# Transposes in two forms: full, or on two row halves, with two PSUM banks each, in a scheduled macaron layer

## Chip, cores and metric

The kernel runs on one core of a Trainium2 chip. The metric is the device time of one execution in microseconds (us); the times shown are medians of several runs. Profiles come from one further execution, recorded by the hardware profiler.

## What is computed

The input x is 8 sequences of 512 tokens and 256 features, in float32. Cut to what matters, the reference is:

```python
def _layer(x, ...):                        # feed-forward half, 2 layers deep
    h = shift_token(x); qkv = h @ wqkv     # 8 heads of 64
    q = l2norm(q) * qs; k = l2norm(k) * ksc; q, k = rotary_xpos(q, k)
    o = local_attention(q, k, v)           # window 128, looks one window back
    x = x + o @ wo
    h = layernorm(shift_token(x)) * lg + lb
    a, g = split(h @ w1 + b1)
    return x + (a * gelu(g)) @ w2 + b2

x = x + 0.5 * ffn(layernorm(x))
x = x + attn(layernorm(x))     # h = LN(x); for each token: y = W q; W -= lr (W k - v) k^T; returns LN(x) + y
x = x + 0.5 * ffn(layernorm(x))
```

Here `ffn` applies `_layer` twice. The same `ffn` weights serve both halves.

## The kernel before

Tokens lie on the 128 partitions: a sequence is four tiles of 128 tokens by 256 features. For each of the 8 sequences and each half and layer, a tile w of x is normalised where a norm is due, transposed on TensorE so that features lie on the partitions (`h.turn`, two 128x128 transposes into one PSUM bank), copied to SBUF (`h.copy`, `hT`), and multiplied with wqkv (L690 for q and k, L777 for v). q and k are rotated (L734, L740, L746) and transposed head by head (`qk.turn`, L801), scores are made (L841), exponentials and shares taken (L896, L917), the shares transposed (`pr.turn`, L943), weighed with v (L980) and projected (L1031). The feed-forward step shifts tokens by DMA into `hs`, normalises two tiles together, transposes them with four 128x128 transposes into one bank (`hn.turn`), spreads them to `h2T` with a scale and a bias on ScalarE (L1102), and multiplies with w1 (L1124) and w2 (L1215, L1226). Between the halves, `ttt` solves the token recurrence in blocks; its normalised rows go through `zn.turn`, two transposes, and a spread (L1304).

All three turns (`h.turn`, `hn.turn`, `zn.turn`) come from one helper, `transposes`, whose instructions all have line L638. There are 128 + 64 + 32 = 224 such steps with 576 transposes in all.

TensorE works in one of three forms, which the code calls kinds: `full` (all 128 rows and columns), `rows` (two halves of 64 rows that work side by side, each into a bank of its own: `qk.turn`, `pr.turn`, L1226 and some steps of `ttt`) and `quad` (four quarters of 64x64: scores, weighing, and the blocks of L1424). The turns of L638 are `full`.

Nothing runs in the order of the source. Each step becomes a `Node` with engine, cost, kind, the buffers that it takes (`Val`, from pools; the pool `ps` is the eight PSUM banks) and those that it uses. `Scheduler.run` (L361) then writes out the instructions of all engines, one node after the other: of all nodes that are ready and for which `room` finds free buffers, it takes the one with the smallest time by its own costs, less a tuned head start (`EARLY` by name, and a pseudo-random one by `VARIED`, one number for each 10 us of TensorE's clock). A node may name several engines (`copy` on ACT or DVE), and then the scheduler picks one; a change of TensorE's kind has its own costs (`PE_DRAIN`, `PE_LOAD`). A value with a `mate` gets two neighbouring banks where it can, and `both_of` returns a view of both. Each engine executes its own instructions in the order written.

At the start, `load_x` (L495) loads a sequence's x; that of sequence 0 goes in four pieces of one tile each, the first ahead of the identity `sq`. The weights' rope tables are multiplied with the scales (L536), each product on DVE or POOL, whichever the scheduler picks; it picked one on each.

Of the kernel before, what the change touches and what calls it, by code (L numbers as in the profile page):

```python
# [112 lines left out]
def t_pool(n, spread=False):  # L113
# [5 lines left out]
    "XT": 400,  # L119
    "XT6": 200,  # L120
    "_full_quad": 850,
    "_full_rows": 350,
    "_quad_full": 400,
    "_quad_rows": 450,
    "_rows_full": 500,
    "_rows_quad": 650,
    "_table": -250,
    "base.x": -700,
    "base.y": 50,
    "base.z": -550,  # L130
    "below": -250,
    "block": 1000,
    "bx": 500,
    "bx.copy": -450,
    "bx6": 1000,
    "bx6.copy": -1000,
    "cross.mask": 2000,
    "down": -300,
    "exp": -950,
    "g": 1000,  # L140
    "gate": 400,
    "gelu": -450,
    "gram": -50,
    "gram.copy": -750,
    "h.copy": -1650,
    "h.edge": 2100,
    "h.turn": 200,
    "h2T": -800,
    "hn": 350,
    "hn.turn": 250,  # L150
    "hs.rstd": -1350,
    "hs.stats": 100,
    "hs.zero": -400,
    "k.scale": 2350,
    "keys": -200,
    "keys.copy": -300,
    "kq": 5100,
    "kq.copy": -1000,
    "last": 200,
    "last.gelu": -650,  # L160
    "least": -250,
    "norm 0": 100,
    "norm 1": 400,
    "ones": 2100,
    "po": 3300,
    "po.add": 50,
# [3 lines left out]
    "pred": 500,  # L170
# [4 lines left out]
    "qk.power": -1650,  # L175
    "qk.square": -550,
    "qk.sum": -550,
    "qk.swapped": 2800,
    "qk.turn": 5050,
    "recip": 950,  # L180
    "remains": 650,
    "rest": -200,
    "rope": -2950,
    "sc": 2350,
    "sequence 4": 350,
    "shares": -50,
    "start": 1000,
    "tv": 2350,
    "u": 5500,
    "u.copy": -100,  # L190
    "v": -50,
    "value": 150,
    "w": 4650,
    "w.add": 350,
    "x.ffn": 200,
    "x.rstd": -1900,
    "x.scale": -500,
    "x.stats": 500,
    "xbx": 2650,
    "xbx.t": 500,  # L200
    "xbx6": 1000,
    "y": 300,
    "z.rstd": -400,
    "z.scale": 50,
    "z.stats": 5600,
    "zT": -450,
    "zero": -1000,
    "zn.rstd": -1850,
    "zn.scale": -350,
    "zn.stats": -500,  # L210
    "zn.turn": 4500,
# [6 lines left out]
    11724, 1019, 59022, 40675, 27471, 54517, 926, 43545, 2398, 24437, 2885, 26297, 23063, 34949,  # L218
    37569, 50685, 32060, 45684, 31371, 39512, 521, 25144, 9512, 57341, 52812, 27993, 489, 16985,
    33884, 26540, 4908, 18540, 8984, 2421, 40841, 59716, 24566, 55621, 54901, 36686, 11720, 16862,  # L220
    12513, 52674, 46515, 10256, 59276, 45325, 19184, 55405, 46136, 42422, 0, 49317, 40524, 44024,
    17428, 31920, 9589, 43511, 59281, 2218, 23017, 28209, 39306, 27771, 33355, 29993, 985, 13712,
    12640, 23397, 12680, 25585, 54109, 44131, 30596, 53412, 59847, 58748, 23508, 2544, 28302, 26557,
    42944, 35720, 53117, 52196, 48722, 45182, 35154, 35344, 11332, 52827, 37344, 43276, 41480,
    25425, 12724, 27463, 8460, 45364, 1608, 2076, 43844, 20601, 2037, 2469, 59305, 53718, 46665,
    7337, 2226, 52207, 33281, 58457, 21599, 41269, 26533, 7438, 10800, 59668, 36328, 9166, 3745,
    46520, 33573, 21192, 14896, 27355, 52409, 47920, 36060, 3581, 40705, 14777, 12200, 5106, 3270,
    51090, 49236, 40806, 56120, 57783, 44110, 54754, 7737, 4795, 57152, 33780, 10581, 19156, 33936,
    14061, 55609, 27768, 30248, 49510, 51041, 20100, 12337, 22860, 5369, 43128, 56887, 21496, 42396,
    49657, 59934, 54949, 51695, 25315, 48261, 6245, 14319, 39121, 50043, 51556, 33881, 37401, 54689,  # L230
    49233, 9924, 153, 33064, 19456, 55060, 55649, 39006, 35496, 52294, 57662, 8411, 23088, 13299,
    21788, 20784, 0, 45292, 52752, 9077, 52413, 35269, 49088, 4635, 56036, 34956, 34764, 55744,
    11631, 10468, 37148, 21711, 44697, 28554, 26398, 22219, 1471, 23536, 6706, 44201, 48828, 45578,
    39704, 45276, 44363, 20013, 25017, 14320, 36906, 53273, 39761, 9386, 19064, 51436, 46401, 15636,
    47446, 53601, 57004, 17096, 7331, 58485, 46128, 47692, 33874, 15433, 23706, 38397, 0, 31180,
    20101, 11661, 56899, 1609, 28145, 25749, 31949, 39204, 1318, 18757, 46711, 24881, 52292, 1629,
    38037,
# [57 lines left out]
class Node:  # L295
    def __init__(self, name, groups, prio, eng, cost, emit, deps, takes, uses, kind, tail, port):
        self.name, self.early = name, sum(EARLY.get(k, 0.0) for k in (name, *groups))
        self.groups, self.key = groups, zlib.crc32(f"{name} {prio[0]}".encode())
        self.prio, self.cost, self.emit, self.takes, self.kind = prio, cost, emit, takes, kind
        self.engs = eng if isinstance(eng, tuple) else (eng,)  # L300
        self.costs = cost if isinstance(cost, tuple) else (cost,)
        self.uses, self.next, self.ready, self.tail, self.port = uses, [], None, tail, port
        self.banks = [v for v in self.uses if v.tag == "ps"]
        self.left = 0
        for d in deps:
            d.next.append(self)
            self.left += 1
        self.deps = deps
        for v in uses:
            v.users += 1  # L310


class Scheduler:
# [47 lines left out]
    def run(self):  # L361
        ready = [n for n in self.nodes if n.left == 0]
        left = len(self.nodes)
        while left:
# [3 lines left out]
            for n in ready:  # L368
# [5 lines left out]
                for eng, cost in zip(n.engs, n.costs):  # L374
# [4 lines left out]
                    if eng == "PE":  # L379
                        t += PE_LOAD[n.kind]  # L380
                        if self.pe_kind not in (n.kind, None):
                            now += PE_DRAIN[self.pe_kind] + PE_LOAD[n.kind]
                            turn = f"_{self.pe_kind}_{n.kind}"
                    elif eng == "ACT" and n.kind and n.kind != self.table:
# [3 lines left out]
                    key = (t - early + EARLY.get(turn, 0.0) + (cost if len(n.engs) > 1 else 0.0), n.prio)  # L388
                    if best is None or key < best[0]:
                        best = (key, n, eng, cost, t, turn)  # L390
            assert best, f"no node can go: {left} left, " + str({k: len(v) for k, v in self.free.items()})
            _, n, eng, cost, t, turn = best
            ready.remove(n)
            left -= 1
            n.ran = eng
# [7 lines left out]
            if eng == "PE":  # L403
                self.pe_kind = n.kind
            if eng == "ACT" and n.kind:
                self.table = n.kind
# [16 lines left out]
def macaron_kernel(ctx: ExitStack, tc: tile.TileContext, a: dict, out: bass.AP):  # L423
# [71 lines left out]
    def load_x(b, w=None):  # L495

        if not w:
            lane[b], first_x[b] = Val("lane"), Val("x")
        own = slice(0, NW) if w is None else slice(w, w + 1)
        order[0] += 1  # L500
        n = node(
# [3 lines left out]
            1500.0 if w is None else 790.0,  # L505
            lambda e: dma(first_x[b].ap[:, own, :], a["x"][b].rearrange("(w p) d -> p w d", p=P)[:, own, :]),
            takes=[] if w else [lane[b], first_x[b]],
            uses=[first_x[b]] if w else [],
            tail=2200.0,
        )  # L510
        L["x", b] = [n] * NW if w is None else [*L.get(("x", b), []), n]
# [8 lines left out]
    def load_layer(l):  # L520
        wqkv = wpool.tile([P, 2, 3 * INNER], F32, name=f"wqkv{l}")
        load(("qk", l), (wqkv[:, :, 0 : 2 * INNER], split(a["wqkv"][l][:, 0 : 2 * INNER])))
        if l == 0:
# [10 lines left out]
            ("DVE", "POOL"),  # L534
            (t_dve(4 * NW * DH), 2400.0),
            lambda e: (nc.vector if e == "DVE" else nc.gpsimd).tensor_tensor(  # L536
# [1220 lines left out]
```

## Time and profile before

| what | value |
|---|---|
| median of 3 runs | 2679.28 us (2678.38 to 2680.19) |
| profiled execution, its own time | 2681.69 us |
| its span | 2679.9 us |
| TensorE busy (PE) | 98% of the span |
| DVE / ACT / POOL busy | 69% / 62% / 58% |
| granted TensorE clock, mean | 0.999 |
| L638, all turns: busy time and count | 44.8 us for the 256 of x, 40.9 us for the 256 of hs, 12.2 us for the 64 of the recurrence's rows |
| L801, turns of q and k on row halves | 91.8 us, 2048 instructions |

The span runs from the first to the last instruction of the program; the rest of the execution's time lies around it. PE is TensorE's matmuls and transposes, PEld its weight loads, DVE the vector engine, ACT the scalar engine, POOL GpSimd, SP the engine that issues the DMAs. An fp32 matmul of the program appears as two instructions in the trace, a transpose as one. Durations of neighbouring matmuls overlap, so their mean is longer than the time from one start to the next. In a row of the order of time, "[0.57 <-DVE row L1556]" means that the engine was idle for 0.57 us until DVE's work on `row` at L1556 was done.

### The profile page before, as it was taken

How to read it: one execution, taken by the hardware profiler on the slowest of the kernel's cores; microseconds unless marked ns; L12 is line 12 of the kernel's file. 1: busy time of each engine (PE TensorE's matmuls, PEld its weight loads, DVE VectorE, ACT ScalarE, POOL GpSimd, SP SyncE). 2: the span in 40 equal slices, each digit the busy share in tenths (PEclk: the TensorE clock that was granted, in tenths of full speed). 3: DMA queues.
4: the chain of work that ended last, by engine and by line, in shares of the span. 5: the costliest groups of instructions: out<-in, count | busy, mean ns of one | idle time of the engine just before them, and what ended most of it. 6: DMA issues, size and time to landing. Idle time of an engine off the chain costs nothing.

```text
span 2679.9 us, 75965 instructions
## 1 busy us (share of the span) xinstructions
PE 2635.3 (98%) x30128; PEld 1995.6 (74%) x30128; DVE 1846.5 (69%) x5571; ACT 1650.8 (62%) x4342; POOL 1543.8 (58%) x2153
## 2 busy tenths in 40 slices
PE   8999999999999999999999999999999999999998
PEld 4777777777767777777777777777777777777776
DVE  6767757765777667766776777776777756776755
ACT  5666665755666666666565666657656656556554
POOL 7655655654576466656565656457556645456633
PEclk9999999999999999999999999999999999999999
DMA  5000000000100000000000000000010000000000
GB/s 184 9 9 16 7 6 17 11 6 6 32 6 10 8 24 17 8 8 9 8 29 8 10 9 24 18 8 8 9 30 8 10 7 8 9 24 8 8 13 17
DMA packets 58554, 44.61 MB, mean 17 GB/s; under 512 B 7468, under 2 KB 55768, under 8 KB 58200
## 3 DMA queue, kind: packets, MB, share of 16 engines
q1 hardware_dynamic: 58200, 39.77, 4.8%
q8 instruction: 237, 3.88, 0.6%
q14 instruction: 117, 0.96, 0.1%
HBM read 18.79 MB, written 4.19 MB: 9 GB/s over the span
## 4 chain that ended last, share of the span: by engine, by line
PE 92%; DVE 2%; DMA 2%; POOL 2%; ACT 1%; issue 1%; SPq 0%; DVEq 0%; POOLq 0%; ACTq 0%
PE ps L1124 22%; PE ps L690 17%; PE ps L1215 9%; PE ps L1031 8%; PE ps L777 8%; PE ps L841 6%; PE ps L980 6%; PE ps L943 4%; PE ps L801 3%; PE ps L638 3%; PE ps L1424 2%; PE ps L1226 1%; PE ps L1336 1%; DMA hs<-x 1%; PE ps L1568 1%
## 5 line engine op out<-in xcount | busy, mean ns | idle before, releaser
L1124 PE MATMUL ps<-h2T,w 128*128 128x256 f32 (+1 forms) x2816 | 646.1, 381 | 2.6 <-DVE gT L1165 1.3
L1124 PEld LDWEIGHTS ps<-h2T,w 128*128 128x128 f32 (+1 forms) x2816 | 521.3, 188 | 122.5 <-issue 30.6
L690 PE MATMUL ps<-wqkv,hT 128*128 128x512 f32 x1024 | 490.2, 603 | 1.4 <-DVE x L1349 1.1
L896 ACT ACTIVATE pr<-pr,s 128x192 f32<-128x192 f32 (+1 forms) x1024 | 440.4, 433 | 49.9 <-DVE s L884 45.8
L917 POOL TENSOR_TENSOR pr<-pr,s 128x384 f32<-128x384 f32 (+1 forms) x375 | 293.5, 790 | 283.9 <-DVE s L909 260.8
L726 POOL TENSOR_TENSOR st<-st,powc 128x8 f32<-128x8 f32 x256 | 438.2, 1712 | 21.3
L884 DVE CUSTOM_DVE_ANT_0 pr<-ps,amask,st 128x192 f32<-128x192 f32 (+1 forms) x1024 | 360.8, 394 | 44.4 <-PE ps L841 36.0
L911 POOL TENSOR_TENSOR s<-s,powc 128x2 f32<-128x2 f32 x189 | 133.7, 708 | 342.5 <-ACT pr L896 341.2
L1165 DVE SCALAR_TENSOR_TENSOR gT<-ps,b,gl 128x256 f32<-128x256 f32 x320 | 151.0, 482 | 219.6 <-PE ps L1124 189.1
L690 PEld LDWEIGHTS ps<-wqkv,hT 128*128 128x128 f32 x1024 | 185.4, 191 | 154.5 <-issue 137.0
L1215 PE MATMUL ps<-w,gT 128*128 128x256 f32 x1280 | 291.4, 379 | 0.3 <-DVE s L884 0.3
L1215 PEld LDWEIGHTS ps<-w,gT 128*128 128x128 f32 x1280 | 241.6, 190 | 50.8 <-issue 15.3
L709 ACT ACTIVATE tmp<-ps 128x512 f32<-128x512 f32 x256 | 152.4, 597 | 174.0 <-DVE rot L734 127.0
L734 DVE TENSOR_TENSOR rot<-ps,rt 128x512 f32<-128x512 f32 x256 | 175.7, 688 | 117.4 <-PE ps L690 103.8
L1031 PE MATMUL ps<-wo,oT 128*128 128x256 f32 x1024 | 244.0, 381 | 0.5 <-DVE oT L1024 0.5
L777 PE MATMUL ps<-wqkv,hT 128*128 128x512 f32 x512 | 240.5, 594 | 0.0
L1031 PEld LDWEIGHTS ps<-wo,oT 128*128 128x128 f32 x1024 | 190.7, 190 | 51.2 <-issue 19.2
L602 ACT COPY prT<-ps 128x512 f32<-128x512 f32 (+1 forms) x364 | 176.9, 548 | 58.6 <-PE ps L943 56.5
L1146 ACT ACTIVATE gl<-ps,b 128x256 f32<-128x256 f32 x320 | 140.8, 473 | 105.9 <-PE ps L1124 101.1
L841 PE MATMUL ps<-kT,qT 64*64 64x128 f32 (+1 forms) x7168 | 194.2, 251 | 9.7 <-ACT qT L602 8.3
L980 PE MATMUL ps<-prT,v 64*64 64x128 f32 (+1 forms) x7168 | 197.1, 247 | 6.1 <-DVE prT L602 2.9
L746 POOL TENSOR_TENSOR rot<-rot,tmp 128x512 f32<-128x512 f32 x146 | 185.4, 1273 | 19.6 <-DVE tmp L740 14.8
(123 smaller groups left out, 4372.5 us busy)
## 6 DMA issues: line engine op xcount, KB each, us to landing
hs<-x SPq DMA_DIRECT2D x128, 64.0 KB
hs<-x SPq DMA_DIRECT2D x128, 63.5 KB
base<-in_x_dram SPq DMA_DIRECT2D x8, 512.0 KB
out_dram<-base SPq DMA_DIRECT2D x8, 512.0 KB
w<-in_w_dram SPq DMA_DIRECT2D x6, 640.0 KB
x<-in_x_dram SPq DMA_DIRECT2D x7, 512.0 KB
wqkv<-in_wqkv_dram SPq DMA_DIRECT2D x2, 1024.0 KB
hs<-x SPq DMA_DIRECT2D x96, 0.5 KB
```

The source lines that it names most:

```text
L690: nc.tensor.matmul(pp.ap, hT[w].ap[:, c * P : (c + 1) * P], wqkv[:, c, i * INNER : (i + 1) * INNER], start=(c == 0), stop=(c == 1),)
L726: nc.gpsimd.tensor_tensor(ss, ss, powc[:, 0:HEADS], ALU.pow)
L746: (nc.vector if e == "DVE" else nc.gpsimd).tensor_tensor(rot.ap, rot.ap, tmp.ap, ALU.add)
L777: nc.tensor.matmul(pv.ap, hT[w].ap[:, c * P : (c + 1) * P], wqkv[:, c, 2 * INNER : 3 * INNER], start=(c == 0), stop=(c == 1),)
L841: nc.tensor.matmul(sc[par].ap[half(c), k * 4 * DH + at : k * 4 * DH + at + keys.stop - keys.start], qT.ap[half(par), 2 * g + k, half(c)], ...
L884: nc.vector.tensor_tensor_reduce(out=pr(k, nj), in0=sc.ap[:, k * 4 * DH : k * 4 * DH + nj], in1=amask[:, 0:nj] if w else amask[:, 3 * DH : ...
L896: nc.scalar.activation(pr(k, nj), pr(k, nj), AF.Exp, bias=st.ap[:, k : k + 1], scale=-1.0, accum_out=st.ap[:, 2 + k : 3 + k],)
L917: (nc.vector if e == "DVE" else nc.gpsimd).tensor_tensor(both, both, st.ap[:, 4:6].unsqueeze(2).to_broadcast([P, 2, nj]), ALU.mult)
L980: nc.tensor.matmul(po[r].ap[half(par), k * P + first : k * P + first + cols * DH], v[j].ap[half(r), hd * DH : (hd + 1) * DH], prT.ap[half( ...
L1031: nc.tensor.matmul(py.ap[:, 0:D], oT.ap[:, c, :], wo[:, c, :], start=(c == 0), stop=(c == INNER // P - 1))
L1124: nc.tensor.matmul(dst.ap[0:rows, 0 : 2 * P], w1[:, kc, col : col + rows], h2T.ap[:, kc, :], start=(kc == 0), stop=(kc == 1),)
L1215: nc.tensor.matmul(py.ap[:, 0:D], gT.ap[:, at : at + P], w2[:, c, :], start=(c == 0), stop=False)
```

## The change

1. `transposes` takes two banks as mates and has two ways, `("full", "rows")`. In the full way it issues the same 128x128 transposes, half of them into each bank. In the rows way each transpose becomes two, of 64 rows and 128 columns, into the same columns of the two banks. `Node` holds a list of ways (engine, cost, kind) in place of engines and costs, and `run` picks one when it issues the node; `n.ran` tells which. The readers (`h.copy` and the two spreads) read both banks, in the order that the way asks for, when they are issued.
2. `load_x` loads every sequence in one piece, and the call for sequence 0 now follows the identity's.
3. The rope products are on POOL alone.
4. `EARLY` and `VARIED` have new values, so the order on every engine differs throughout.

In the order that results, 75 of the 224 turns go on row halves: 35 of 128 `h.turn`, 33 of 64 `hn.turn` and 7 of 32 `zn.turn`. The sequences are worked through in the order 4, 3, 7, 0, 2, 5, 1, 6, where it was 4, 0, 1, 2, 3, 6, 7, 5; SP issues the inputs of 7, 3 and 4 first, where it was that of 4, then weights, then the four pieces of 0.

```diff
 EARLY = {
...
-    "_full_quad": 850,
-    "_full_rows": 350,
-    "_quad_full": 400,
-    "_quad_rows": 450,
-    "_rows_full": 500,
-    "_rows_quad": 650,
+    "_full_quad": 1050,
+    "_full_rows": 750,
+    "_quad_full": 250,
+    "_quad_rows": 500,
+    "_rows_full": 450,
+    "_rows_quad": 550,
...
-        self.engs = eng if isinstance(eng, tuple) else (eng,)
-        self.costs = cost if isinstance(cost, tuple) else (cost,)
+        ways = [w if isinstance(w, tuple) else (w,) for w in (eng, cost, kind)]
+        count = max(map(len, ways))
+        self.ways = list(zip(*(w * count if len(w) < count else w for w in ways)))
...
-                for eng, cost in zip(n.engs, n.costs):
+                for way in n.ways:
+                    eng, cost, kind = way
...
-            n.ran = eng
+            n.ran = kind
...
-            lambda e: dma(first_x[b].ap[:, own, :], a["x"][b].rearrange("(w p) d -> p w d", p=P)[:, own, :]),
+            lambda e: dma(first_x[b].ap, a["x"][b].rearrange("(w p) d -> p w d", p=P)),
...
-            ("DVE", "POOL"),
-            (t_dve(4 * NW * DH), 2400.0),
+            "POOL",
+            2400.0,
...
-        def transposes(name, dst, src, deps, takes, uses, n):
-            def emit():
+        def transposes(name, pts, src, deps, takes, uses, n):
+            pts[0].mate = pts[1]
+            def emit(e):
+                out = both_of(*pts)
                 for k in range(n):
-                    nc.tensor.transpose(dst(k), src(k), ident)
-            return pe(name, t_tr(times=n), emit, deps, takes=takes, uses=uses)
+                    if me.ran == "full":
+                        nc.tensor.transpose(out[:, 2 * k // n, 2 * k % n * DH : (2 * k % n + 2) * DH], src(k), ident)
+                    else:
+                        for r in range(2):
+                            rows = slice(r * DH, (r + 1) * DH)
+                            nc.tensor.transpose(out[:, r, k * DH : (k + 1) * DH], src(k)[rows], ident[rows, rows])
+            me = node(
+                name, prio(), "PE", (t_tr(times=n), T_TURN * n), emit, deps, [*pts, *takes], uses, ("full", "rows")
+            )
+            return me
...
+                def turned_x(n=n, pts=pts):
+                    src = both_of(*pts)[:, :, 0:P]
+                    return src if n.ran == "full" else src.rearrange("p r (c t) -> p r c t", c=2)
...
-        load_x(0, 0)
         load("ident", (sq, a["sq"]))
-        for w in range(1, NW):
-            load_x(0, w)
+        load_x(0)
```

## The prediction

> **What bounds the kernel now.** I read the page's engine rows first, then the busy time by stretches, then the order of time on TensorE, in the middle of the run and at its start.
>
> ```profile
> span 2679.9 us, 75965 instructions
> ...
> PE 2635.3 (98%) x30128; PEld 1995.6 (74%) x30128; DVE 1846.5 (69%) x5571; ACT 1650.8 (62%) x4342; POOL 1543.8 (58%) x2153
> ```
>
> TensorE is idle for 2679.9 - 2635.3 = 44.6 us in all, and no other engine is above 69%. So the time is TensorE's own stream plus a few waits. Where the waits lie is in the table of stretches (length, busy time of PE, PEld, DVE, ACT, POOL, then granted clock, DMA share, GB/s):
>
> ```profile
> 0.00:60.00 60.00, 48.01 (x439) 26.68 (x440) 40.09 (x125) 28.63 (x83) 46.79 (x80) 0.97 0.60 203
> ...
> 1200.00:1800.00 600.00, 599.54 (x6868) 457.35 (x6861) 425.96 (x1284) 377.92 (x1002) 338.28 (x468) 1.00 0.05 13
> ...
> 2600.00:2680.00 80.00, 69.77 (x798) 53.88 (x796) 44.76 (x134) 34.54 (x98) 29.77 (x38) 0.98 0.05 15
> ```
>
> The first 60 us hold 12.0 us of idle time; the last matmul ends at 2674.6, so 5.3 us at the end are the last additions and the store; 44.6 - 12.0 - 5.3 = 27.3 us are spread over the body. Next is what the stream is made of (start us, duration, instruction; I subtract starts of neighbours, since durations overlap):
>
> ```profile
> 667.41 0.60 PE L638 MATMUL ps<-sq,x 128*128 128x128 f32 x4
> 667.85 1.88 PE L690 MATMUL ps<-wqkv,hT 128*128 128x512 f32 x4
> ```
>
> ```profile
> 684.82 1.88 PE L690 MATMUL ps<-wqkv,hT 128*128 128x512 f32 x4
> 686.54 1.88 PE L777 MATMUL ps<-wqkv,hT 128*128 128x512 f32 x4
> 688.35 0.46 PE L943 MATMUL ps<-sq,pr 64*128 64x64 f32 x8
> 688.74 1.98 PE L777 MATMUL ps<-wqkv,hT 128*128 128x512 f32 x4
> 690.66 0.66 PE L980 MATMUL ps<-prT,v 64*64 64x128 f32 x16
> ```
>
> Four full transposes take 0.44 us, 0.109 each (the most frequent start-to-start in the records too). Row-half transposes exist already: 16 of L801 take 0.49 us where nothing disturbs them, 0.0307 each, so a whole 128x128 block by two halves costs 0.061. And a change of the array's form costs: the projection at 684.82 takes 1.72 us to its neighbour, the next one, before a step on row halves, 1.81 (0.09 more); the 8 row transposes take 0.39 against 8 x 0.0307 = 0.25 (0.145 more); the projection after them takes 1.92, of which 0.09 is leaving again and 0.10 is for having come in. A full stretch between two tiled ones thus costs 0.09 + 0.145 + 0.10 = 0.34 us beyond its work.
>
> **The change, part by part.** *Transposes in two forms.* The order of the changed program has 224 turn steps as before, 75 of them on row halves: 216 of the 576 full transposes become 432 half ones. Full: 216 x 0.109 = 23.6 us. Halves: 432 x 0.0307 = 13.3 us. Gain 10.3 us, all on TensorE's path. The other bound is the median of a step of 16, 0.548 us or 0.0343 each: 14.8 us, gain 8.8. I take 10.3, since all row turns stand inside stretches that are on row halves already.
>
> *Changes of form.* The new tuning numbers reorder everything. Counted in the two orders: full stretches 223 before, 241 after; direct changes between row halves and quarters 126 before, 129 after. That is 18 x 0.34 = 6.1, and 3 x 0.15 = 0.45: together 6.6 us lost. So the stream gains 10.3 - 6.6 = 3.7 us, not ten.
>
> *Two banks for each turn.* [...] Here all 224 turns take two of eight banks, the full ones too. No row of before shows two-bank x turns; the nearest are the q,k turns of L801, which already fill two banks: their copies cost 588 ns (128x512, ACT) against 587 for a copy from one bank (v), so reading two banks costs nothing and I give the copies and the scaled spreads (L602, L1102, L1304) no change. For waiting, I counted cover: for each TensorE step of the body, the TensorE work that the order puts between the last step it depends on, through other engines or through a buffer or bank, and itself, less the mean durations of the steps between. This is a count by rows, with no queueing in it. Of some 2790 steps, 17 before have less cover than they need, together 6.7 us; after, 33 and 9.6 us. Under half a microsecond of cover have 261 before and 311 after. [...] The count can be held against the trace: three of the 17 are the steps of L1568 in one sequence, 0.45 us short each, and their rows show idle times of 0.57, 0.51 and 0.51:
>
> ```profile
> 643.63 0.70 PE L1568 MATMUL ps<-row,ttta 128*128 128x256 f32 x2 [0.57 <-DVE row L1556]
> ```
>
> The body's 27.3 us should grow by a factor between 311/261 = 1.19 and 9.6/6.7 = 1.43. I take 1.3: 8.2 us more. [...] The bounds are wide: with better places for the waits the body's idle time could also fall by some 5 us, and by the number of uncovered steps (33/17) it could nearly double.
>
> *The first input and the rope product.* The start of before, from the order of time (DVE and POOL rows beside PE):
>
> ```profile
> 4.74 0.43 DVE L621 BATCH_NORM_STATS2 st<-x 128x6 f32<-128x256 f32 x1 [4.74 <-DMA x<-in_x_dram]
> ...
> 7.39 1.12 PE L638 MATMUL ps<-sq,x 128*128 128x128 f32 x4 [7.39 <-DVE x L629]
> ...
> 10.17 5.89 PE L690 MATMUL ps<-wqkv,hT 128*128 128x512 f32 x8
> ...
> 10.42 3.38 POOL L536 TENSOR_TENSOR rt<-gT,ttta 128x1024 f32<-128x1024 f32 x1 [0.34 <-DMA gT<-in_rope_dram]
> ```
>
> ```profile
> 35.60 0.69 PE L801 MATMUL ps<-sq,rot 64*128 64x64 f32 x8 [2.68 <-POOL rot L746]
> ```
>
> Before already loads one whole input first; the four pieces belong to a sequence that starts later and gain nothing here. SP's order after has three whole inputs (1.5 MB) ahead of the identity, the weights, the scales and the rope table. The DMA records show 0.37 MB started per us once full, and 0.7 us from last start to use. So the sequence that is computed first, whose input is third, lands at about 7.5 instead of 4.74, the first weights at 10.3, the rope table at 12.9 (10.3 before). POOL's order puts the four inverse roots of another sequence first (0.87 us each in before's rows), so the first scaling comes at about 10 and the first transposes at 10.5 instead of 7.4. The first projection stands behind three turned tiles: at 12.8 instead of 10.17, 2.6 us late. Both rope products then run on POOL, 3.4 and about 2.4 us (1.2 us of the 3.38 lie beside the one that DVE did), between the roots and the first powers; the first q,k turn would come at about 26.5, as before, with two projection steps (3.4 us) less done. But behind it the new order puts the second q,k turn and the first weighing later, so 2.68 us of wait above and 1.3 us of waits at 42 and 44 us find cover. Following the rows to the first row transposes of the weights I get 40.4 against 41.3, with one score step more done. I take 0 for the start, with bounds of -2 and +3. Eleven input loads become eight; after the start no wait of PE's is put down to a load of x.
>
> *The end.* The last turn of the feed-forward goes on row halves behind a step that is on row halves: 0.25 instead of 0.44 us and a change of form less before the wait: -0.3 us. DVE loses about 29 shares of 0.55 us and 14 additions of 0.72, and gains 29 reciprocals of 0.16 and two dozen copies of about 0.6; POOL gains the shares. Both stay under 70%, so I give that nothing beyond the count of cover.
>
> Sum, against the profiled execution's 2681.69 us (span 2679.9 and 1.8 around it): -10.3 + 6.6 + 8.2 + 0 - 0.3 = +4.2, so 2685.9. The median of the three runs, 2679.28, lies 2.4 below the profiled one: 2683.5, rounded 2684.
>
> **The rivals.** *The stream decides (faster).* The body's waits stay 27.3 us and the start comes out 2 us ahead: -10.3 + 6.6 - 0.3 - 2 = -6.0, 2673. For it: the stream's gain is the surest term, and most waits of before come from queues on DVE, ACT and POOL, which the count leaves out. Against it: every measure of cover moved the other way.
>
> *Banks decide (slower).* With turns holding two banks, gate, projection and output steps (gate 1 and 4, L690 1 and 7, L1031 3 and 7 uncovered steps, before and after) stand behind copies that free a bank. TensorE works in order, so one late step holds all. If idle time follows the number of uncovered steps, 27.3 x 33/17 = 53: +25.7 - 4.0 = +21.7, 2701. From about 9.4 us more idle time on (a factor of 1.34) the result is beyond the 0.2% that a measurement can tell from no change. For it: TensorE is above 98%, so nothing hides a wait. Against it: each shortage in the count is small, a third of a microsecond.
>
> **How the numbers follow.** Likeliest, 0.45: 2684, itself between 2680 and 2688; of this 0.30 is within 0.2% (2673.9 to 2684.6) and 0.15 above. Stream, 0.27: nearly all faster (0.24). Banks, 0.28: slower. So faster 0.24, same 0.33, slower 0.43. The range 2670 to 2701 reaches both rivals.
>
> **What would show it.** In the profile after: row transposes of x near 0.031 us each and full ones still 0.109; PE busy time little changed (the changes of form count as busy); idle time of PE in the body near 35 us (27 speaks for the stream, 50 for banks), with waits on copies out of PSUM before projections and gate steps; the first PE instruction near 10.5 us, and the first 60 us with about 12 us idle. Idle time in the body below 25 us, or a start later by over 5 us, makes the prediction wrong.

## The result and the profile after

The changed kernel takes 2738.59 us (median of 4 runs, 2736.75 to 2742.46) against 2679.45 of before in the same set of runs: ratio 1.0221, 95% interval 1.0206 to 1.0236. It is 2.2% slower. The prediction, 2684, had the sign of its small slowdown right and was 55 us too low; the time lies outside its range of 2670 to 2701. In the runs below, the median of the kernel before lies between 2679.5 and 2681.3 us.

The profiled execution took 2740.23 us. From the page of the kernel after:

```profile
span 2738.3 us, 76345 instructions
...
PE 2655.1 (97%) x30344; PEld 1997.3 (73%) x30344; DVE 1859.9 (68%) x5578; ACT 1631.0 (60%) x4312; POOL 1563.6 (57%) x2168
```

No engine other than TensorE has become the bound. TensorE's idle time is 2738.3 - 2655.1 = 83.2 us, where it was 44.6. The table of stretches (length, busy time of PE, PEld, DVE, ACT, POOL, then granted clock, DMA share, GB/s) shows where:

```profile
0.00:60.00 60.00, 43.47 (x444) 25.00 (x445) 45.04 (x125) 28.15 (x82) 45.01 (x82) 1.00 0.60 203
...
1200.00:1800.00 600.00, 577.99 (x6821) 434.19 (x6818) 408.27 (x1228) 364.56 (x961) 356.81 (x480) 0.99 0.05 13
```

The stretch from 1200 to 1800 us held 0.5 us of idle time and now holds 22.0. The start has 16.5 us where it had 12.0. The rest is spread.

Visible idle time is only part of the waiting, since the modelled ends of matmuls cover some of it. So I took TensorE's records of both kernels apart in another way: time from start to start, less the work at the prices of the rows (0.109 us for a full transpose, 0.0307 for a half one, and so on), less each change of form at the lower quartile of its own kind.

| us | before | after | difference | predicted |
|---|---|---|---|---|
| work by the rows | 2499.4 | 2489.1 | -10.3 | -10.3 |
| changes of form, undisturbed | 99.0 | 105.9 | +6.9 | +6.6 |
| ahead of the first TensorE instruction | 7.4 | 10.4 | +3.0 | 0 for the whole start |
| waits | 68.5 | 127.2 | +58.7 | +8.2 |
| end | 5.6 | 5.8 | +0.2 | -0.3 |

The sum is the difference of the spans. The row of waits is what is left over, so it also holds the waits of the first 60 us and what TensorE loses at half clock. Only the waits are far off.

### The profile page after: what moved, and what is told of

It is laid out like the page before. It is cut to its first block, busy times and chain, and to the rows that moved or that the text cites. A ratio compares the mean times of both kernels' runs of the same rounds, so it can differ in the third digit from the quotient of the medians.

```text
span 2738.3 us, 76345 instructions
## 1 busy us (share of the span) xinstructions
PE 2655.1 (97%) x30344; PEld 1997.3 (73%) x30344; DVE 1859.9 (68%) x5578; ACT 1631.0 (60%) x4312; POOL 1563.6 (57%) x2168
## 4 chain that ended last, share of the span: by engine, by line
PE 86%; DVE 4%; POOL 3%; ACT 3%; issue 2%; DMA 2%; SPq 0%; DVEq 0%; ACTq 0%; POOLq 0%
PE ps L1146 20%; PE ps L706 15%; PE ps L1237 9%; PE ps L1047 8%; PE ps L793 7%; PE ps L857 6%; PE ps L996 6%; PE ps L959 3%; PE ps L817 3%; PE ps L1452 2%; PE ps L638 1%; PE ps L1248 1%; PE ps L1364 1%; DMA hs<-x 1%; DMA x<-in_x_dram 1%
## 5 line engine op out<-in xcount | busy, mean ns | idle before, releaser
L1146 PE MATMUL ps<-h2T,w 128*128 128x256 f32 (+1 forms) x2816 | 650.5, 383 | 11.2 <-DVE x L1056 3.0
L706 PE MATMUL ps<-wqkv,hT 128*128 128x512 f32 x1024 | 494.2, 607 | 1.4 <-ACT hT L596 0.9
L933 POOL TENSOR_TENSOR pr<-pr,s 128x384 f32<-128x384 f32 (+1 forms) x404 | 313.1, 783 | 312.5 <-DVE s L925 299.2
L706 PEld LDWEIGHTS ps<-wqkv,hT 128*128 128x128 f32 x1024 | 184.7, 191 | 155.1 <-issue 133.4
L927 POOL TENSOR_TENSOR s<-s,powc 128x2 f32<-128x2 f32 x160 | 111.9, 700 | 287.7 <-ACT pr L912 284.7
L762 POOL TENSOR_TENSOR rot<-rot,tmp 128x512 f32<-128x512 f32 x160 | 205.9, 1292 | 41.2 <-DVE tmp L756 33.5
L857 PEld LDWEIGHTS ps<-kT,qT 64*64 64x64 f32 x7168 | 172.3, 134 | 43.0 <-ACT qT L596 16.2
L996 PE MATMUL ps<-prT,v 64*64 64x64 f32 (+1 forms) x7168 | 197.2, 247 | 4.9 <-ACT prT L596 2.3
```

Source lines behind the costliest of these rows:

```text
L706: nc.tensor.matmul(pp.ap, hT[w].ap[:, c * P : (c + 1) * P], wqkv[:, c, i * INNER : (i + 1) * INNER], start=(c == 0), stop=(c == 1),)
L762: (nc.vector if e == "DVE" else nc.gpsimd).tensor_tensor(rot.ap, rot.ap, tmp.ap, ALU.add)
L857: nc.tensor.matmul(sc[par].ap[half(c), k * 4 * DH + at : k * 4 * DH + at + keys.stop - keys.start], qT.ap[half(par), 2 * g + k, half(c)], ...
L933: (nc.vector if e == "DVE" else nc.gpsimd).tensor_tensor(both, both, st.ap[:, 4:6].unsqueeze(2).to_broadcast([P, 2, nj]), ALU.mult)
L996: nc.tensor.matmul(po[r].ap[half(par), k * P + first : k * P + first + cols * DH], v[j].ap[half(r), hd * DH : (hd + 1) * DH], prT.ap[half( ...
L1146: nc.tensor.matmul(dst.ap[0:rows, 0 : 2 * P], w1[:, kc, col : col + rows], h2T.ap[:, kc, :], start=(kc == 0), stop=(kc == 1),)
```

## What the trace shows of the new waits

I followed each wait of TensorE back to the first step that was late. Three kinds stand out.

**Copies out of two banks that are far apart.** In the order of time of the kernel after (TensorE and ScalarE rows), a turn of `hs` on row halves ends at 451.8, and ScalarE's copy ahead (of `oT`, not shown) at 454.1:

```profile
451.39 0.43 PE L642 MATMUL ps<-sq,hs 64*128 64x64 f32 x8
...
455.94 0.71 PE L817 MATMUL ps<-sq,rot 64*128 64x64 f32 x16
456.70 1.02 ACT L1124 ACTIVATE h2T<-ps,lnp 128x256 f32<-128x256 f32 x2 [2.62 <-PE ps L817]
457.61 0.58 ACT L596 COPY prT<-ps 128x512 f32<-128x512 f32 x1
...
458.25 0.56 PE L996 MATMUL ps<-prT,v 64*64 64x128 f32 x16 [1.59 <-ACT prT L596]
```

The spread to `h2T` starts 2.6 us after both, at the end of L817, a q,k turn of another sequence. Nothing in the kernel's own lists ties them. But the turn of `hs` got the banks 0 and 7, and that q,k turn the banks 1 and 2. Behind the spread wait the copy of `prT` and then TensorE, 1.59 us.

`Scheduler.slots` gives a pair two neighbouring banks where two are free, and any two otherwise (`or pairs`); `both_of` then returns one view with a stride from the one to the other. For every copy out of two banks I counted how much later it starts than its data and its engine allow, taking delays over 0.15 us. In the kernel after, 408 copies out of neighbours are late by 1.7 us in all, 56 out of banks that lie 2 to 7 apart by 46.5 us. In the kernel before, which has such pairs for the q,k turns alone, it is 1.0 us for 236 copies and 15.8 us for 20. That makes 47 late copies out of distant pairs in the two kernels, and 45 of them start within 0.15 us of the end of the last step on a bank *between* the two. In 35 of the 45 that step is TensorE's, which writes the bank; in the other 10 it is a step of VectorE or ScalarE that reads it. The kernel before shows it plainly:

```profile
893.81 0.76 PE L801 MATMUL ps<-sq,rot 64*128 64x64 f32 x14
894.49 0.90 PE L980 MATMUL ps<-prT,v 64*64 64x128 f32 x32
...
895.69 0.83 PE L980 MATMUL ps<-prT,v 64*64 64x128 f32 x28
896.59 0.59 ACT L602 COPY kT<-ps 128x512 f32<-128x512 f32 x1 [2.35 <-PE ps L980]
...
897.71 1.55 PE L841 MATMUL ps<-kT,qT 64*64 64x128 f32 x47 [1.20 <-ACT qT L602]
```

The keys are turned by 894.6, in banks 0 and 6, but their copy starts at the end of L980, at 896.5. Here is one in the kernel after that VectorE's reading of a bank between holds:

```profile
1121.85 0.58 ACT L596 COPY kT<-ps 128x512 f32<-128x512 f32 x1 [2.54 <-DVE gT L1187]
```

It is the program that makes these copies wait, by its semaphores (counters that one engine raises and another waits for). As built, 46 of the 47 late copies carry a wait for the count that the last step on a bank between raises. The copy of the keys at 896.59 waits for TensorE's count 6094, which L980 gives from bank 5, though the turn itself had ended with 6058.

**VectorE in front of late transfers.** TensorE's longest wait, from the order of time of the kernel after (SyncE, VectorE and TensorE rows):

```profile
1416.73 0.54 SPq L1705 DMA_DIRECT2D out_dram<-base  x1
...
1421.30 0.39 SPq L1677 DMA_DIRECT2D base<-in_x_dram  x1
...
1421.74 0.50 SPq L502 DMA_DIRECT2D x<-in_x_dram  x1
...
1425.25 1.10 DVE L1688 SCALAR_TENSOR_TENSOR base<-x,base 128x256 f32<-128x256 f32 x3 [5.51 <-DMA base<-in_x_dram]
...
1428.90 0.47 PE L638 MATMUL ps<-sq,x 128*128 128x128 f32 x1 [5.43 <-DVE x L623]
```

The reload of `base` can't be issued before the store of `base` has left, 4.6 us after it; the next x stands behind it on SyncE. VectorE's instructions start in the program's order (all 5578 of them in this trace), and its next step needs the reload, so it is idle for 5.51 us with the norm of the next sequence behind. Two more places look alike, at 736.7 (3.04 us of TensorE) and 2438.9 (3.70). VectorE's idle time put down to reloads of `base` rose from 2.7 to 10.9 us. A further loss follows, as two stretches of TensorE around this wait show:

```profile
1420.60:1427.40 6.80, 2.87 (x14) 1.00 0.49 155
1427.44:1434.27 6.83, 5.37 (x38) 0.50 0.00 1
```

In the 6.83 us from 1427.44 us on, the first 1.46 of which still belong to the wait, the granted clock is 0.50. Four projections (L706, at 1431.41) take 3.38 us there, where four take 1.88 at full clock. By the granted clock, 0.50 against 1.00, the 5.37 us of work would take half, so this stall costs an estimated 2.7 us more.

**Table loads.** Of ScalarE's 174 loads of an activation table in the kernel after, 24 did not run ahead while their activation waited for data (12 of 182 before). The wait came first: these loads began only when the data came, with 40.1 us (11.2) of idle time in front. Most of the new ones belong to the last, narrow GELU of a block (L1207).

## The experiments

Theories at the outset: BANKS (a second bank per turn makes TensorE wait), ORDER (the new tuning numbers give a worse order), START. Later, from the section above: SPAN (copies wait for steps on the banks between), TRANSFERS (VectorE waits in front of a late transfer) and TABLES (table loads that wait for data).

Most kernels here keep one order: the choice in `Scheduler.run` is replaced by a list of (step, engine, form) read from the plan of one of the two kernels, so that one thing can be changed with all else in place. Where a buffer isn't free in time, the next step of the list that can go goes first.

```diff
-            for n in ready:
...
+            for place, (at, code) in enumerate(plan[0:400]):
+                n = self.nodes[at]
+                if n.left == 0 and self.room(n) is not None:
+                    break
```

**First set.** `turn_banks` returns one value or two, by a list of turns.

```diff
-                hT[w], pts = Val("hT"), [Val("ps"), Val("ps")]
+                hT[w], pts = Val("hT"), turn_banks("h.turn")
```

*before_2bank*: before's order, two banks for all 224 turns, all full.

> The order of before, kept as a fixed list, with every turn of x and of the norms' rows taking two PSUM banks, in the full form only (no row halves); a few steps shift where a bank is not free. It adds no TensorE work; changes of form stay at 223 full stretches. Theory BANKS (a second bank per turn is what makes TensorE wait): the waits grow by about as much as from before to after, so 2715 to 2740 us. Theory ORDER (the waits come from the newly packed order, the banks by themselves cost little): 2679 to 2695 us, most of it by the steps whose work is not ready in time, which rise from 17 to 71 in the planner's own count.

Measured 2748.02 us (ratio 1.0256, 1.0240 to 1.0271). That is 8 us above the range of BANKS and 53 above that of ORDER.

*before_edge*: before's order, `"rows"` for 22 turns beside a stretch on row halves, two banks for those.

> The order of before with 22 of its 224 turns, those that stand beside a stretch on row halves already, done on row halves in two banks; all others full in one bank; x of the first sequence loaded in one piece. By the rows of the two forms the turns give back about 2.5 us and three full stretches fewer 1.0 us: 3.5 us less TensorE work. Theory ORDER: the waits stay as in before, so about 2676 us. Theory BANKS: 22 of 224 turns hold a second bank, a tenth of 58 us of waits or 6 us: about 2682 us. Anything above 2690 would say that the form itself costs time that neither counts.

Measured 2682.18 us (1.0004, 0.9998 to 1.0011). There is no gain from 3.5 us less work, as BANKS had it.

*after_1bank*: after's order, one bank for the 149 full turns.

> The order of after, kept as a fixed list, with the 149 full turns written to one PSUM bank instead of two; the 75 on row halves keep two. TensorE work and changes of form as in after. Theory BANKS: the waits for a bank that the trace of after shows beyond before's (13 us, with what it leaves unattributed up to 23 us) go: 2716 to 2726 us. Theory ORDER: the order is what makes data late, one bank less per turn takes away only some bank waits: 2730 to 2738 us.

Measured 2736.49 us. Only 2 us come back, and the single runs overlap with those of after, which speaks for ORDER. The first set contradicts itself, unless an order that isn't made for two banks pays in one way and an order that is pays in another.

*after_start*: after's order with the start mended.

```diff
-load.x 7, load.x 3, load.x 4, weights
+load.x 4, weights, load.x 7, load.x 3
```

> The order of after with the start mended: the inputs of the second and third sequence are loaded behind the first layer's weights, their norms held back behind the first q and k work, the first layer's rope table on VectorE. First 60 us of after: TensorE busy 43.5 us where before has 48.0. Theory START (a tenth of the loss is made there and stays): 3 to 5 us come back, 2734 to 2736 us. If what is won at the start is lost at the next wait: 2738 to 2740 us.

Measured 2742.67 us, a miss. The first TensorE instruction comes at 7.04 instead of 10.37 us, but the new start makes a wait of its own of 5.41 us at 29.4, and 10.24 us at half clock follow it. START is not shown, and what the start costs by itself stays open beyond the 3.0 us ahead of the first instruction.

**Second set.** *after_reload*: after's order, five steps moved.

```diff
+load.x 5
 store 7
 again 2
-load.x 5
...
-base.x 2 (three steps)
 x.stats 5
 x.scale 5
...
+base.x 2 (three steps)
```

The second place is mended by moving `load.x` of sequence 0 ahead of the store of sequence 4.

> The order of after as a fixed list, with five steps moved in the two places where VectorE waits longest for a transfer in front of a stall of TensorE (at 734 to 739 us and at 1420 to 1425 us): the load of the next x stands ahead of the store that ends a sequence, not behind that store and the reload after it, and three base additions, which wait for the reload, stand behind the statistics of the new sequence. Nothing else moves. Theory TRANSFERS (VectorE held in front of a late transfer holds TensorE, and the idle time then costs a window at half clock): the stalls of 5.4 and 3.0 us and what the half-clock windows behind them cost (some 2.7 and 1.7 us) go: 2725 to 2729 us. Theory BANKS or GIVEN BACK (the time is lost at the next wait in any case): 2735 to 2739 us.

Measured 2729.44 us (1.0175, 1.0160 to 1.0191): 9.2 us less. At the same place, from its order of time:

```profile
1411.66 0.54 SPq L1586 DMA_DIRECT2D out_dram<-base  x1
1412.25 0.49 SPq L374 DMA_DIRECT2D x<-in_x_dram  x1
...
1417.93 0.43 DVE L487 BATCH_NORM_STATS2 st<-x 128x6 f32<-128x256 f32 x1 [3.25 <-DMA x<-in_x_dram]
...
1420.13 0.44 PE L519 MATMUL ps<-sq,x 128*128 128x128 f32 x2 [1.72 <-DVE x L495]
```

x is issued 0.6 us behind the store instead of 5.0, and TensorE waits 1.72 us instead of 5.43. TRANSFERS is shown.

*after_full*: after's order, `kind` `"full"` for all turns, two banks each.

> The order of after as a fixed list, two banks for every turn as in after, but all 224 turns in the full form. By the rows that is 10.3 us more of transposes, 42 full stretches more (14.3 us) and 30 fewer changes between row halves and quarters (-4.5 us): 20 us more work on TensorE. If the work decides: 2755 to 2760 us. If much of it falls into waits that are there anyway: 2742 to 2750 us. If the form on row halves were itself what costs the time: below 2735 us.

Measured 2740.97 us: 20 us more work by the rows cost 2.4 us, within the spread of the runs. Part of the reason is that a full turn of `hs` is spread from one bank at a time: in this kernel the spreads out of distant pairs are not late at all, and the copies out of all such pairs are late by 27.2 us instead of 46.5. Another part, which the fourth set separates, is that work falls into waits.

*before_plain* and *after_plain*: the two kernels with their planners as they are, but `VARIED = []`.

> The kernel before with the second tuning table (the variation by stretches) emptied, so that its planner decides by costs and the first table alone. One half of a pair. Full stretches 266, direct changes 136: 43 x 0.34 + 10 x 0.15 = 16 us of work more than before. Theory TUNING (both kernels lose about alike without the table; the loss of the change is in how well its order was tuned): 2760 to 2800 us, and the other half of the pair within 20 us of it. Theory STRUCTURE (two banks and the second form cost waits in any order): this one 2760 to 2780 us, and the other half 50 us or more above.

> The kernel after with the second tuning table emptied, the other half of the pair. Work by the rows: full stretches 312, direct changes 153, 202 transposes' blocks on row halves: 46 x 0.34 + 17 x 0.15 - 9.7 = 8 us more than the first half. Theory TUNING: within 20 us of the first half of the pair, work included. Theory STRUCTURE: 50 us or more above it.

Measured 2745.74 and 2781.28 us. Both lose by it (65 and 43 us), and they lie 35.5 us apart, between the theories. In after_plain the copies out of distant pairs are late by 25.6 us; before_plain has one such pair and no late copy.

**Third set.** The bank numbers are chosen anew, all else kept, so that all pairs are neighbours; the list comes from a search through the plan.

```diff
-                now = sorted((s for s in free if s[0] <= t), key=lambda s: s[0])
...
-                    pairs = [(s, at[s[3] + 1]) for s in now if s[3] + 1 in at] or pairs
...
+                k = next(self.banks)
+                v.slot = next(s for s in free if s[3] == k)
```

*before_fixed* is the control: before's order as a list, x of the first sequence in one piece.

> The order of before as a fixed list, every turn full and in one bank; only x of the first sequence is loaded in one piece, as in after. The control for all kernels that keep before's order, and the change's smallest part by itself. Every theory: within 2 us of before, 2678 to 2682 us.

Measured 2682.43 us (1.0006, 0.9997 to 1.0015). The list adds nothing that can be told apart, nor does the load.

> The order of before as a fixed list, with nothing changed but the numbers of the PSUM banks: they are chosen anew so that the two banks of every q,k turn are neighbours; before has 10 of 128 whose two banks lie 2 to 7 apart. In the trace of before the copies out of such pairs start 15.8 us later in all than their data and their engine are ready, those out of neighbours 1.0 us. Theory SPAN (a copy that reads two banks which are not neighbours waits also for what is written into the banks between them): about 8 us of it stood in TensorE's way, 2671 to 2675 us. Theory ROOM (the number of banks held decides, not where they lie): no change, 2678 to 2682 us.

*before_near* measured 2667.06 us (0.9955, 0.9942 to 0.9967): 13.8 us **faster** than before and below the 2671 to 2675 of SPAN, from nothing but bank numbers. The place shown above, in its order of time:

```profile
890.66 0.75 PE L692 MATMUL ps<-sq,rot 64*128 64x64 f32 x14
891.34 0.90 PE L871 MATMUL ps<-prT,v 64*64 64x128 f32 x32
891.46 0.58 ACT L462 COPY kT<-ps 128x512 f32<-128x512 f32 x1 [0.37 <-PE ps L692]
```

The copy of the keys now starts when the turn ends, beside the weighing (L871, which was L980), and not behind it.

> The order of after as a fixed list, only the bank numbers chosen anew: the two banks of all 352 turns are neighbours, where after has 48 pairs that are not. In the trace of after the copies out of those start 46.5 us late in all, those out of neighbours 1.7 us. Theory SPAN: 15 to 20 us come back on TensorE, 2719 to 2724 us. Theory ROOM: the same number of banks is held for the same steps, 2735 to 2739 us.

*after_near* measured 2706.90 us (1.0104, 1.0088 to 1.0119): 31.7 us less than after. ROOM is refuted here, since the same number of banks is held by the same steps. The `h2T` spread of the first fence:

```profile
454.00 0.37 ACT L462 COPY oT<-ps 128x256 f32<-128x256 f32 x1 [0.47 <-PE ps L871]
454.26 1.03 ACT L999 ACTIVATE h2T<-ps,lnp 128x256 f32<-128x256 f32 x2
...
455.17 0.59 ACT L462 COPY prT<-ps 128x512 f32<-128x512 f32 x1
...
456.87 0.90 PE L871 MATMUL ps<-prT,v 64*64 64x128 f32 x32
```

It follows the copy ahead of it at once; `prT` is there in time, and TensorE's weighing does not wait.

> Both mendings together on after's order: neighbouring banks for all turns, and the five steps moved that waited for late transfers. If the two causes are separate their gains add: 9 us less than the kernel with neighbouring banks alone, about 2710 to 2715 us by SPAN and TRANSFERS. If they share the same waits: 2717 us or more.

*after_near_reload* measured 2695.86 us: 11.0 us less than after_near. The two causes add. Not all of the 11.0 need be the mended waits: after_near's profile has 17.1 us at half clock ahead of its last matmul, 10.2 of them away from the two mended places, and this one's has none.

**Fourth set.** 28.8 us between after_near_reload and before_near were open: the second bank as such, the row form, or the order.

> The order of before as a fixed list, every turn full and in two banks, as in the run that took 2748.0 us, but with bank numbers chosen so that the two banks of all 352 turns are neighbours; in that run 68 pairs were not, and the copies out of them started 80 us late in all. Theory SPAN (most of what a second bank costs is these copies): 2680 to 2700 us. Theory ROOM (holding a second bank in an order not made for it costs time wherever it lies): 2715 to 2735 us.

> The order of after as a fixed list, all turns full in two banks that are neighbours. Against the same with 75 turns on row halves (2706.9 us) it has by the rows 20 us more work on TensorE (10.3 of transposes, 9.8 of changes of form). If that work decides: 2722 to 2728 us. If the form on row halves is worth little even without spanning copies, since the work falls into waits: 2708 to 2714 us.

> The order of after alone: all turns full and in one bank, as in before, with the q,k turns in neighbouring banks. It differs from before with neighbouring banks (2667.1 us) only in the order of the steps, with 60 full stretches more and 27 fewer changes between row halves and quarters: 16 us more work, and 3 us at the start. If the rest of the loss is in the second bank: about 2690 us. If it is in the order (waits for transfers, table loads and data): 2715 to 2725 us.

> The order of before as a fixed list, 22 turns beside a stretch on row halves done on row halves in two banks, and all two-bank turns in neighbouring banks. Work by the rows: 3.5 us less than with full turns only (2667.1 us). If the form on row halves brings what its rows say: 2663 to 2665 us. If the second bank of 22 turns eats it: 2666 to 2670 us.

*before_2bank_near* measured 2713.14 us, *after_full_near* 2712.25, *after_order* (`turn_banks` gives one bank to all) 2713.38, *before_edge_near* 2669.64 (0.9956, 0.9943 to 0.9968). The first lies between the ranges of SPAN (2680 to 2700) and ROOM (2715 to 2735), so in before's order the place of the second bank and the holding of it both cost time. With the runs above, in us:

| order, and banks of a turn | as the planner places them | all pairs neighbours |
|---|---|---|
| before, one, full | 2682.4 | 2667.1 |
| before, two, full | 2748.0 | 2713.1 |
| after, one, full | not run | 2713.4 |
| after, two, full | 2741.0 | 2712.3 |
| after, two, 75 turns on row halves | 2738.6 | 2706.9 |

Along each row, distant pairs cost 15, 35, 29 and 32 us. Down the right column, a second bank costs 46 us in the order that was not made for it and nothing that can be measured in the order that was; but that order costs 46 us in itself. Each of the two costs 46 us alone, and both together cost no more. The row form is worth some 5 us in after's order (the intervals overlap), a quarter of what its rows say. In before's order, where its 22 turns also take a second bank, it gains nothing.

**Fifth set.** *after_gelu*: after_near_reload with ten steps moved on ScalarE.

```diff
-last.gelu, gelu, gelu
+gelu, gelu, last.gelu
```

> The kernel with after's order, neighbouring banks and the five steps moved (2695.9 us), with one thing more: in ten places the GELU of the last, narrow gate step is moved on ScalarE behind the one or two GELUs of its block that were ready before it. In the trace those ten table loads began 0.6 to 3.0 us after ScalarE was free, 18 us in all, each at the moment when the last gate step ended. Theory TABLES (a table load waits for the data of the activation behind it, and holds ScalarE meanwhile): 3 to 5 us come back, 2691 to 2693 us. Rival (ScalarE's waits lie beside other work): 2695 to 2697 us.

Measured 2691.06 us (1.0039, 1.0026 to 1.0051), against 2695.86 (1.0043 to 1.0070). One place, first in after_near_reload, then in after_gelu:

```profile
841.40 1.28 ACT L1082 ACT_TABLE_LOAD   x1 [2.95 <-PE ps L1021]
842.70 0.47 ACT L1082 ACTIVATE gl<-ps,b 42x256 f32<-42x256 f32 x1
843.19 0.84 ACT L1043 ACTIVATE gl<-ps,b 128x256 f32<-128x256 f32 x2
```

```profile
839.31 1.28 ACT L1043 ACT_TABLE_LOAD   x1
840.60 0.84 ACT L1043 ACTIVATE gl<-ps,b 128x256 f32<-128x256 f32 x2
842.25 0.47 ACT L1082 ACTIVATE gl<-ps,b 42x256 f32<-42x256 f32 x1 [0.81 <-PE ps L1021]
```

The load moves in front of the wait, and ScalarE's idle time before table loads falls from 41.9 to 23.7 us. What TensorE gets of it is not settled: the medians are 4.8 us apart, the intervals overlap, and the profiled spans (2690.2 and 2689.2) differ by 1.0.

*after_plain_near*: after_plain's order as a list, with all pairs neighbours.

> The kernel after with the second tuning table emptied (2781.3 us), its order kept as a fixed list and only the bank numbers chosen anew, so that all 352 pairs are neighbours; in its trace the copies out of the 40 pairs that are not start 25.6 us late in all. SPAN at the rate of after (32 of 46.5): 18 us less, 2763 us. Against the kernel before without the table (2745.7 us), 11 us of the difference are work and start by the rows. Theory TUNING: what is left beyond that is under 10 us, so an order for two banks is hardly poorer by nature. Theory ROOM: the time stays above 2775 us.

Measured 2756.74 us: 24.5 us less. What is left against before_plain is 11.0 us, as much as the 8 of work and 3 at the start by the rows. Without the second table the second bank and the second form cost no more than their work.

## Why the prediction was wrong

From before to after by measured steps, one way of two: 2680.8 - 13.8 (before without distant pairs) + 46.3 (after's order) - 1.1 (second bank) - 5.4 (row form) + 31.7 (distant pairs) = 2738.5. So of the change's 58 us, 18 are distant pairs, net of what before already paid for them, and 40 are the new order with its second banks, which cost 46 and whose row form gives 5 back. How the 46 fall to the order and to the banks depends on the way: with the second bank first (before_2bank_near) the bank costs 46 us, and the order then takes 1 off. In after's order, an estimated 19 of the 46 are form changes and start by the rows (without row turns the order has 60 full stretches more than before, 27 direct changes fewer); the row form's own rows came out at a quarter, so this share is not shown. Mending late transfers gave 11.0 us back in after_near, mending the GELUs behind that 1 to 5. The rest, 11 to 15 us, are waits that I did not trace.

**The step that failed** is the one on two banks, together with the term of the waits that rests on it: +8.2 us, where the waits grew by 58.7. It says "reading two banks costs nothing and I give the copies ... no change". It took the price of a second bank from the *duration* of L801's copies, 588 ns against 587. The durations were right and still are. What two banks can cost is the *start*: 10 of those 128 pairs lay apart, and 13 of their copies started late, 15.8 us in all. Those rows were in the trace of before, one of them with 2.35 us of idle time and TensorE's own 1.20 us behind it. At the rate of before, which the later run gave as 13.8 us for 10 pairs, the 48 pairs of the change would cost 66 us, where 31.7 were measured. That is twice too much, but it would have said that the term is not nothing. The right sign was in part luck: the waits did decide, but mostly by causes that the count of cover does not hold.

*Body waits.* +8.2 was mis-sized in three ways. By the prediction's own sign, TensorE's idle time in the body, it is 83.2 less 16.5 at the start and 5.5 at the end, or 61.2 us, where about 35 was forecast and 50 stood for banks. Its base of 27.3 us was visible idle time, where the waits are 68.5. Its factor of 1.3 came from a count of cover that knows the listed dependencies and buffers, no distant pairs, no late transfer, no table load that waits; the waits grew by a factor of 1.86. And it had no term for the half clock, which held for 20.5 us in the body of after and not at all in the body of before (its one such window, 3.4 us at 35.3, lies in the start).

*Transposes by halves, -10.3, and form changes, +6.6.* Both right as work (-10.3 and +6.9). They are not right as time: where TensorE waits anyway, 20 us of such work by the rows were worth 5.

*Start, 0.* The events fell as worked out: first TensorE instruction at 10.37 (10.5), first projection at 12.66 (12.8), first q,k turn at 26.90 (26.5). What failed is the cover behind them: the second q,k turn waits too, and the first turn of the weights' shares came at 44.7 instead of 40.4.

```profile
26.90 0.46 PE L817 MATMUL ps<-sq,rot 64*128 64x64 f32 x8 [0.96 <-POOL rot L777]
29.75 0.46 PE L817 MATMUL ps<-sq,rot 64*128 64x64 f32 x8 [2.39 <-DVE rot L762]
```

*End, -0.3.* It measured +0.2, within what one trace can tell.

*The rivals.* "Banks decide" had the right sign and place in the chip, PSUM, and for the largest part of it that was traced, the distant pairs, the wrong mechanism: it put the wait on steps that need a free bank. Waits put down to a bank not yet free rose from 9.4 to 22.7 us, and giving a bank back in after's order returned 2 us. In before's order a second bank for every turn cost 46 us with all pairs neighbours (2713.1 against 2667.1), though its turns are all full. No run shows that holding the second bank itself slows the kernel after; what is shown there is what the planner does when neighbours are not free. "The stream decides" fell with the waits.

*Open.* Whether the tuning could find an order for two banks as good as before's. after_plain_near suggests that nothing in the structure forbids it, for one pair of first tables. The version that beats both kernels is before_near, 2667.1 us.

## What to carry to other kernels

Price a wider operand by when its readers start, not only by how long they take; a rare pattern in the trace of before (10 pairs of 128) tells what a change pays that makes it common. In a program built like this one, a view with a stride over PSUM banks ties its reader to the other engines' steps on the banks between (46 of the 47 late copies here), so keep pairs adjacent or read each bank by itself. In a stream that one engine bounds at 98%, a gain in work is real only where that engine doesn't wait (here 20 us of it by the rows were worth 5), and an order that is tuned for one set of buffers is part of the cost of changing them.

## What the runs showed of the hardware

The late copies out of distant banks are no sign of how the chip reads PSUM: 46 of the 47 carry a semaphore wait for the step between. The copies themselves take as long as from one bank (588 ns against 587 before).

In the body of the kernel after, the granted clock fell to 0.50 four times: for 3.41 us from 741.37 and from 1205.58 us on, and for 6.83 us from 1427.44 and from 2441.20 us on. Each fall comes during one of TensorE's four longest idle times of the body, or 1.6 us behind it (741.37): 3.04 us (up to 739.75), 2.35 us (up to 1205.77), 5.43 us (up to 1428.90) and 3.70 us (up to 2442.62). The starts lie 464.21, 221.86 and 1013.76 us apart; divided by 136, 65 and 297 that is 3.413 us each, the length of the two shorter falls. The length of an idle time alone does not tell whether the clock falls: 2.35 us was enough at 1205.58, while after the 2.39 us up to 29.75 us it stayed at 1.00. In the 3.41 us ahead of each of the four starts TensorE was 47, 37, 0 and 33% busy; in the two stretches of that length that hold the 2.39 us (24.57 to 27.98 and 27.98 to 31.40 us) it was 54 and 48% busy. These few cases give no rule: before_2bank fell to half clock at 403.59 us with no idle time of 1.9 us near it.

A table load takes 1.28 us, in each of the 182 of the kernel before and the 174 of the kernel after. ScalarE's median idle time before a load is 0.02 us, and behind it 0.01, in both.
